# A re-ordered beginning for a four-layer graph network kernel on one core

## Chip, cores and metric

The kernel runs on one core of one Trainium2 chip. The metric is the device time of that core in microseconds (us), smaller is better. PE is TensorE (matmul), PEld its weight loads, DVE VectorE, ACT ScalarE, POOL GpSimd, SP SyncE; "SPq" and "ACTq" are the DMA queues that the sync engine and ScalarE issue to.

## The reference, cut to what matters

The input is 128 graphs of 128 nodes with 256 features. Four layers follow each other, each `x = layernorm(x + layer(x))`:

```python
x = _layernorm(x + L0(x, W_lin, W_val, a, W_out, adj, src, dst))   # attention over 512 edges
x = _layernorm(x + L1(x, adj, W1, W2, W3))                         # three mixes over adj * adj
x = _layernorm(x + L2(x, W, adj, bias))                            # diagonal, upper, lower part
x = _layernorm(x + L3(x, adj, ...))                                # batch norm over all graphs

# L0, for all graphs:
Xq = (H @ W_lin.T).reshape(bt, n, h, dh);  Xv = (H @ W_val.T).reshape(bt, n, h, dh)
e  = einsum('behd,hd->beh', leaky_relu(Xq[:, src] + Xq[:, dst]), a) + log(A0[src, dst] + EPS)
# softmax of e over the edges of equal src; then a sum over the edges of attn * Xv[:, dst], @ W_out.T
```

The edge list is the same for all graphs, so everything that depends on it alone is computed once: the **edge constants** (the order of the edges sorted by source, the gather indices, the log weight of each edge, the marks of repeated edges).

## The kernel before: the parts that matter

Graphs are processed in quads of four (32 quads). A quad's chain for layer 0 is: `values_in` (transposes), `values` (products with `wqv`, stored to DRAM as `qd`), `gather` (eight indirect DMAs on GpSimd, four plain ones by source, four that add by destination), `score` (VectorE), `softmax_parts` (four scans on VectorE), `attention`, `scatter` (four indirect DMAs, then a load of the whole attention matrix `ad`), `by_row` (copies on ScalarE) and `stage_a` (layer 0's matmuls and norm). A loop turn does stages of five different quads, in a fixed order of instructions per engine; ahead of the loop, the chains of quads 0 and 1 must have been run. In the code ahead of the loop the compiler's scheduler chooses the order; in the loop the written order is kept.

```python
a_sb = cload([P, N], "adj", adj)
xg0 = load_x(0, "xg", 1)
wqv = cload(...)
...
values_in(0, xg0)
for i in range(QB):
    values(0, i)
with tc.tile_pool(name="set", bufs=1) as sp:      # edge constants, in scratch memory of their own
    ...                                           # two 1 MB zero stores, ranks, permutation
    src_idx, dst_idx = ...                        # sorted gather indices
    ends_row = ...                                # the sorted ends, spread over all partitions
    for c in range(NE):                           # pairs of edges, on the sorted order
        nc.vector.tensor_scalar(same[:, c, :], pair_row, pair_col[:, c:c + 1], None, op0=ALU.is_equal)
        nc.vector.scalar_tensor_tensor(prior[:, c, :], ...)
        nc.vector.scalar_tensor_tensor(less[:, c, :], ...)
    nc.vector.reduce_sum(again, prior, axis=AX.X)
    ...                                           # log_row; adjacency: wt_t, split_t, diag_bc, ahat_t
cst2 = phase.enter_context(tc.tile_pool(name="cst2", bufs=1))
wo = cload(...); w1_sb = cload(...); w2_sb = cload(...); w3_sb = cload(...); l2w = cload(...) # 5.1 MB
...
gather(0)
edges(0)            # score and softmax of quad 0
whole(1)            # values_in and values of quad 1
attention(0)
scatter(0)
gather(1)
edges(1)
attention(1)
whole(2)
...
for j in range(QB):
    by_row(0, j)
scatter(1)
gather(2)
stage_a(0)          # layer 0 of quad 0
mix1(0, 0); mix1(0, 2); first(0, 0)
for i in range(QB): ... # first(0, i + 1), mix2(0, i)
with tc.manual_schedule(engines=None):
    for k in range(NQ + 1):
        iteration(k)
```

Of the kernel before, what the change touches and what calls it, by code (L numbers as in the profile page):

```python
# [19 lines left out]
BIG = 1e38  # L20
# [4 lines left out]
def gnn_stack(ctx: ExitStack, tc: tile.TileContext, x, adj, w_qv_t, a, w_out_t, src, dst,  # L25
# [80 lines left out]
    with ExitStack() as phase:  # L106
# [13 lines left out]

        a_sb = cload([P, N], "adj", adj)
        xg0 = load_x(0, "xg", 1)
        wqv = cload([P, DC, 2 * D], "wqv", w_qv_t.rearrange("(c p) f -> p c f", p=P))
        a_bc = cload([P, D], "a_bc", bass.AP(tensor=a.tensor, offset=a.offset, ap=[[0, P], [1, D]]), nc.scalar)

# [7 lines left out]
        log_row = ctile([R, E], "log_row", pool=cst)  # L133
# [11 lines left out]
        def values_in(k, xg=None):  # L145

            s = quads[k]
            s.xts = []
            xg = load_x(k, "xg", 1) if xg is None else xg
            for j in range(0, QB, 2):  # L150
                pt = ps("pt").rearrange("p (b c n) -> p b c n", b=2, c=DC)
                for t in range(2):
                    for c in range(DC):
                        nc.tensor.transpose(pt[:, t, c, :], xg[:, j + t, c * P:(c + 1) * P], ident)  # L154
                xt = ws.tile([P, 2, DC, P], F32, tag="xt", name="xt")
                nc.vector.tensor_copy(xt, pt)  # L156
                s.xts.append(xt)

        def values(k, i):

            s = quads[k]
# [7 lines left out]
            nc.vector.tensor_copy(s.xv[:, i, :], pq[:, D:])  # L169
            if i == QB - 1:  # L170
                s.qd = q_dram[k % 4]
                nc.sync.dma_start(s.qd, s.qt.rearrange("p b d -> p (b d)"))

        def gather(k):

            s = quads[k]
            s.z = [ws.tile([P, QB * D], F32, tag="zs", name=f"zs{k}_{c}", bufs=NE) for c in range(NE)]
            for idx, op in ((src_idx, ALU.bypass), (dst_idx, ALU.add)):
                for c in range(NE):
                    nc.gpsimd.indirect_dma_start(out=s.z[c], out_offset=None, in_=s.qd,  # L180
                                                 in_offset=bass.IndirectOffsetOnAxis(ap=idx[:, c:c + 1], axis=0),
                                                 compute_op=op)

        def score(k, c):
# [8 lines left out]
            nc.vector.reduce_sum(s.es[:, c, :], z.rearrange("p (r d) -> p r d", d=DH), axis=AX.X)  # L193

        def softmax_parts(k):
# [5 lines left out]
            e = wk.tile([R, E], F32, tag="e", name="e", bufs=1)  # L201
            nc.vector.tensor_add(e, log_row, pe[:R, :])
            yield
            f = wk.tile([R, E], F32, tag="f", name="f", bufs=1)
            nc.vector.tensor_tensor_scan(f, reset_f, e, initial=0.0, op0=ALU.add, op1=ALU.max)
# [5 lines left out]
            nc.vector.tensor_sub(e, e, m)  # L211
# [206 lines left out]


        values_in(0, xg0)  # L420
        for i in range(QB):
            values(0, i)
        with tc.tile_pool(name="set", bufs=1) as sp:
            src_col = cload([P, NE], "src_col", src.rearrange("(c p) -> p c", p=P), nc.scalar, I32, sp)
            dst_col = cload([P, NE], "dst_col", dst.rearrange("(c p) -> p c", p=P), nc.scalar, I32, sp)
            src_row = cload([P, E], "src_row", bass.AP(tensor=src.tensor, offset=src.offset, ap=[[0, P], [1, E]]),
                            nc.scalar, I32, sp)
            ones = ctile([P, P], "ones", pool=sp)
            nc.vector.memset(ones, 1.0)
            zero = ctile([P, N * R], "zero", pool=sp)  # L430
            nc.gpsimd.memset(zero, 0.0)
            for ad in att_dram:
                nc.scalar.dma_start(ad[:N * N, :].rearrange("(t s) r -> t (s r)", s=N), zero)


            pos = ctile([P, E], "pos", pool=sp)
            nc.gpsimd.iota(pos, pattern=[[1, E]], base=0, channel_multiplier=0,
                           allow_small_or_imprecise_dtypes=True)
            pos_col = ctile([P, NE], "pos_col", pool=sp)
            nc.gpsimd.iota(pos_col, pattern=[[P, NE]], base=0, channel_multiplier=1,  # L440
                           allow_small_or_imprecise_dtypes=True)
            ends = ctile([P, 2, NE], "ends", pool=sp)
            nc.vector.tensor_copy(ends[:, 0, :], src_col)
            nc.vector.tensor_copy(ends[:, 1, :], dst_col)
            key_row = ctile([P, E], "key_row", pool=sp)
            nc.vector.tensor_copy(key_row, src_row)
            nc.vector.scalar_tensor_tensor(key_row, key_row, float(E), pos, op0=ALU.mult, op1=ALU.add)
            key_col = ctile([P, NE], "key_col", pool=sp)
            nc.vector.scalar_tensor_tensor(key_col, ends[:, 0, :], float(E), pos_col, op0=ALU.mult, op1=ALU.add)

            less = ctile([P, NE, E], "less", pool=sp)
            rank = ctile([P, NE], "rank", pool=sp)
            perm = ctile([P, NE, E], "perm", pool=sp)
            bcast = ctile([P, 2, NE, P], "bcast", pool=sp)
            for c in range(NE):
                nc.vector.tensor_scalar(less[:, c, :], key_row, key_col[:, c:c + 1], None, op0=ALU.is_lt)
            nc.vector.reduce_sum(rank, less, axis=AX.X)
            for c in range(NE):
                nc.vector.tensor_scalar(perm[:, c, :], pos, rank[:, c:c + 1], None, op0=ALU.is_equal)
                for t in range(2):  # L460
                    nc.vector.tensor_copy(bcast[:, t, c, :], ends[:, t, c:c + 1].to_broadcast([P, P]))


            pc = ps("pcol")[:, :NE * 2].rearrange("p (c t) -> p c t", t=2)
            for c in range(NE):
                for i in range(NE):
                    nc.tensor.matmul(pc[:, c, :], perm[:, i, c * P:(c + 1) * P], ends[:, :, i],
                                     start=(i == 0), stop=(i == NE - 1))
            cols = ctile([P, NE, 2], "cols", pool=sp)
            nc.vector.tensor_copy(cols, pc)  # L470
            nc.vector.tensor_copy(src_idx, cols[:, :, 0])
            nc.vector.tensor_copy(dst_idx, cols[:, :, 1])

            ends_row = ctile([P, 2, E], "ends_row", pool=sp)
            for t in range(2):
                pr = ps("ends_ps")
                for c in range(NE):
                    nc.tensor.matmul(pr, bcast[:, t, c, :], perm[:, c, :], start=(c == 0), stop=(c == NE - 1))
                nc.vector.tensor_copy(ends_row[:, t, :], pr)


            pair_row = ctile([P, E], "pair_row", pool=sp)
            nc.vector.scalar_tensor_tensor(pair_row, ends_row[:, 1, :], float(N), ends_row[:, 0, :],
                                           op0=ALU.mult, op1=ALU.add)
            pair_col = ctile([P, NE], "pair_col", pool=sp)
            nc.vector.scalar_tensor_tensor(pair_col, cols[:, :, 1], float(N), cols[:, :, 0],
                                           op0=ALU.mult, op1=ALU.add)
            same = ctile([P, NE, E], "same", pool=sp)
            prior = ctile([P, NE, E], "prior", pool=sp)
            for c in range(NE):  # L490
                nc.vector.tensor_scalar(same[:, c, :], pair_row, pair_col[:, c:c + 1], None, op0=ALU.is_equal)
                nc.vector.scalar_tensor_tensor(prior[:, c, :], pos, pos_col[:, c:c + 1], same[:, c, :],
                                               op0=ALU.is_lt, op1=ALU.mult)
                nc.vector.scalar_tensor_tensor(less[:, c, :], pos, pos_col[:, c:c + 1], same[:, c, :],
                                               op0=ALU.is_gt, op1=ALU.mult)
            again = ctile([P, NE], "again", pool=sp)
            nc.vector.reduce_sum(again, prior, axis=AX.X)
            nc.vector.tensor_scalar(again, again, 0.5, None, op0=ALU.is_gt)
            spare = ctile([P, NE], "spare", pool=sp)
            nc.vector.scalar_tensor_tensor(spare, pos_col, float(N * N), pair_col, op0=ALU.add, op1=ALU.subtract)  # L500
            nc.vector.tensor_mul(spare, spare, again)
            nc.vector.tensor_add(spare, spare, pair_col)
            nc.vector.tensor_copy(att_idx, spare)
            count = ps("count")
# [289 lines left out]
```

## Time and profile before

| | before |
|---|---|
| median of 4 runs | 3486.15 us (3485.91 to 3490.95) |
| span of the profiled run, mean granted clock | 3483.9 us, 0.968 |
| busy: PE, DVE, ACT, POOL | 95%, 52%, 28%, 16% |
| first L314 matmul (loop proper starts) | 156.51 us |
| first split_t matmul of turn 1 (L359) | 230.42 us |

The prediction below shows and reads the table of stages, the matmul engine's waits and the queue lines. This is VectorE's timeline of the kernel before, with cuts. A row of a timeline is: start, length, engine, line, operation, tiles, shapes, count, and in brackets the idle time just before it with what ended it.

### The profile page before, as it was taken

The page shows a single profiled execution, that of the slowest core. Times are in us where ns is not written, and L with a number is a line of the kernel's source. Part 1 is how long each engine was busy: PE and PEld are TensorE (multiplying, and loading weights), DVE is VectorE, ACT ScalarE, POOL GpSimd, SP SyncE. Part 2 cuts the span into 40 slices and gives each one's busy share as a digit, 9 for nine tenths or more (in the row PEclk, how much of TensorE's full clock was granted, in tenths as well). Part 3 has the DMA queues.
Part 4 walks back from the last instruction along what each step waited for, and adds up shares of the span by engine and source line. Part 5 has one row for each costly group of instructions (what it writes and reads, how often), then busy time and mean ns, then how long its engine had stood idle before and what let it go on. Part 6 is the DMA issues. An engine that isn't in the chain of part 4 may idle for free.

```text
span 3483.9 us, 33805 instructions
## 1 busy us (share of the span) xinstructions
PE 3303.1 (95%) x13130; PEld 2105.6 (60%) x13130; DVE 1797.1 (52%) x3549; ACT 974.6 (28%) x1637; POOL 543.6 (16%) x460
## 2 busy tenths in 40 slices
PE   5599999999999999999999999999999999989963
PEld 2366666666666666666666666666666666654442
DVE  6544455555554555554445554555545553233379
ACT  1122222222222222222222222222222222234452
POOL 3211111111111111111111111111111110000000
PEclk8799999999999999999999999999999999999975
DMA  6433333323222233333333323322233331034446
GB/s 201 120 86 97 85 97 97 97 79 97 89 83 74 83 91 98 97 98 97 91 92 97 97 82 94 93 82 78 75 91 97 97 91 37 19 123 173 157 132 224
DMA packets 127743, 347.78 MB, mean 100 GB/s; under 512 B 14432, under 2 KB 68576, under 8 KB 115040
## 3 DMA queue, kind: packets, MB, share of 16 engines
q0 software_dynamic: 40960, 135.29, 16.1%
q1 hardware_dynamic: 65168, 190.53, 15.3%
q10 hardware_dynamic: 21456, 19.81, 1.7%
q8 instruction: 104, 1.70, 0.2%
q14 instruction: 55, 0.45, 0.0%
HBM read 258.55 MB, written 87.03 MB: 99 GB/s over the span
## 4 chain that ended last, share of the span: by engine, by line
PE 91%; DVE 4%; DMA 2%; issue 1%; ACT 0%; POOL 0%; DVEq 0%; POOLq 0%; ACTq 0%; SPq 0%
PE ph L314 25%; PE p L325 13%; PE po L373 10%; PE po L728 6%; PE ph L412 6%; PE ph L294 6%; PE pq L167 6%; PE pm L304 3%; PE po L269 3%; PE pm L359 3%; PE py L260 2%; PE pa L398 2%; PE pm L280 2%; PE po L336 2%; DVE x3l L98 1%
## 5 line engine op out<-in xcount | busy, mean ns | idle before, releaser
L314 PE MATMUL ph<-m,w 128*128 128x512 f32 x2048 | 887.2, 594 | 3.9 <-DVE m L305 3.9
L314 PEld LDWEIGHTS ph<-m,w 128*128 128x128 f32 x2048 | 390.5, 191 | 481.6 <-issue 476.0
L325 PE MATMUL p<-w,h 128*128 128x256 f32 x2048 | 450.4, 381 | 0.0
L325 PEld LDWEIGHTS p<-w,h 128*128 128x128 f32 x2048 | 387.1, 190 | 52.2 <-issue 0.5
L180 POOL DMA_INDIRECT zs<-qd,src_idx x128 | 126.5, 989 | 1797.6 <-DVE f L214 1571.8
L373 PE MATMUL po<-l2w,ms 128*128 128x256 f32 x1536 | 347.6, 379 | 1.2 <-DVE ms L365 1.2
L317 ACT ACTIVATE h<-ph 128x512 f32<-128x512 f32 x256 | 152.8, 597 | 598.6 <-PE ph L314 598.6
L373 PEld LDWEIGHTS po<-l2w,ms 128*128 128x128 f32 x1536 | 284.6, 190 | 35.9 <-DVE ms L365 1.4
L294 PE MATMUL ph<-w,mx 128*128 128x512 f32 x512 | 235.7, 593 | 0.0
L167 PE MATMUL pq<-wqv,xt 128*128 128x512 f32 x512 | 231.1, 605 | 2.9 <-DVE xt L156 2.9
L728 PE MATMUL po<-zl,l3w 128*128 128x512 f32 x512 | 221.9, 597 | 10.5 <-ACT zl L723 10.5
L412 PE MATMUL ph<-ag,l3w 128*128 128x512 f32 x512 | 225.5, 593 | 0.3 <-ACT ag L401 0.3
L180 POOL DMA_INDIRECT zs<-qd,dst_idx x128 | 202.8, 1584 | 121.5 <-DMA zs<-qd,src_idx 101.4
L338 DVE TENSOR_TENSOR xr<-xr,po 128x512 f32<-128x512 f32 x64 | 43.7, 683 | 336.5 <-PE po L336 336.5
L90 ACT ACTIVATE ln_sd<-ln_mv,eps 128x2 f32<-128x2 f32 x256 | 75.4, 294 | 456.5 <-DVE ln_mv L85 449.9
L156 DVE COPY xt<-pt 128x512 f32<-128x512 f32 x64 | 41.4, 685 | 310.1 <-PE pt L154 310.0
L236 POOL DMA_INDIRECT attd<-at,att_idx x128 | 127.5, 996 | 440.4 <-DMA attd<-at,att_idx 283.4
L98 DVE TENSOR_SCALAR xr<-xr,ln_mv,ln_rs 128x256 f32<-128x256 f32 x384 | 179.7, 510 | 6.9
L728 PEld LDWEIGHTS po<-zl,l3w 128*128 128x128 f32 x512 | 98.1, 192 | 134.3 <-issue 112.2
L190 DVE SCALAR_TENSOR_TENSOR zs<-zs 128x1024 f32<-128x1024 f32 x128 | 155.6, 1216 | 35.2 <-DMA zs<-qd,dst_idx 35.2
L412 PEld LDWEIGHTS ph<-ag,l3w 128*128 128x128 f32 x512 | 96.9, 190 | 121.6 <-issue 112.3
L167 PEld LDWEIGHTS pq<-wqv,xt 128*128 128x128 f32 x512 | 97.2, 195 | 115.1 <-issue 110.4
(173 smaller groups left out, 3965.4 us busy)
## 6 DMA issues: line engine op xcount, KB each, us to landing
ad<-attd SPq DMA_DIRECT2D x32, 1024.0 KB, 4.7
zd<-z SPq DMA_DIRECT2D x32, 1024.0 KB, 7.3
zl<-zd SPq DMA_DIRECT2D x32, 1024.0 KB, 4.8
xg<-in_x_dram SPq DMA_DIRECT2D x32, 512.0 KB, 4.2
qd<-qt SPq DMA_DIRECT2D x32, 512.0 KB, 2.6
xr<-in_x_dram SPq DMA_DIRECT2D x32, 512.0 KB, 5.8
x3d<-xr SPq DMA_DIRECT2D x32, 512.0 KB, 2.9
x3l<-x3d SPq DMA_DIRECT2D x32, 512.0 KB, 4.4
```

The costliest lines, as they stand in the source:

```text
L98: nc.vector.tensor_scalar(r[:, i, :], r[:, i, :], mv[:, i, 0:1], rs[:, i:i + 1], op0=ALU.subtract, op1=ALU.mult)
L167: nc.tensor.matmul(pq, s.xts[i // 2][:, i % 2, c, :], wqv[:, c, :], start=(c == 0), stop=(c == DC - 1))
L180: nc.gpsimd.indirect_dma_start(out=s.z[c], out_offset=None, in_=s.qd, in_offset=bass.IndirectOffsetOnAxis(ap=idx[:, c:c + 1], axis=0), com ...
L190: nc.vector.scalar_tensor_tensor(z, z, SLOPE, z, op0=ALU.mult, op1=ALU.max)
L236: nc.gpsimd.indirect_dma_start(out=ad, out_offset=bass.IndirectOffsetOnAxis(ap=att_idx[:, c:c + 1], axis=0), in_=s.at[:, c, :], in_offset= ...
L294: nc.tensor.matmul(ph, s.mx[i // 2 * 2][:, i % 2, dc, :], w1_sb[:, dc, :], start=(dc == 0), stop=(dc == DC - 1))
L314: nc.tensor.matmul(ph, w2_sb[:, c, f * P:(f + 1) * P], s.m2[:, c].rearrange("p b n -> p (b n)"), start=(c == 0), stop=(c == K1 - 1))
L317: nc.scalar.activation(h.rearrange("p b n -> p (b n)"), ph, AF.Relu)
L325: nc.tensor.matmul(p3[:, t * D:(t + 1) * D], s.h2[f][:, j + t, :], w3_sb[:, f, :], start=(f == 0), stop=(f == K2 - 1))
L373: nc.tensor.matmul(po[:, i % 2, :], mss[i][:, t, dc, :], l2w[:, t, dc, :], start=(n3 == 0), stop=(n3 == 3 * DC - 1))
L412: nc.tensor.matmul(ph, l3w1[:, dc, c * P:(c + 1) * P], s.ag[:, dc, :], start=(dc == 0), stop=(dc == DC - 1))
L728: nc.tensor.matmul(po, w2t[:, c, o * P:(o + 1) * P], z[:, c, :], start=(c == 0), stop=(c == K3 - 1))
```

## The change

The intent: run the start in an order written by hand (`start()` inside the manual schedule), with each load issued when it is needed. The edge constants are computed on the edges in their original order with accumulating compares, and only the needed results are sorted. Gather 0's eight pieces are interleaved, each add close behind its source piece, where the kernel before issues all four source pieces first. Quad 1's and quad 2's values run early, quad 3's leave turn 0, and layer 0 of quad 0 is placed ahead of the end of quad 1's chain. In the softmax an add of the log weights to the 16x512 scores becomes an add to the 128x64 ones, and in the loop the softmax steps stand at other places among the value products.

```diff
+        xg0 = load_x(0, "xg", 2)
+        wqv = cload(...)
         a_sb = cload([P, N], "adj", adj)
-        xg0 = load_x(0, "xg", 1)
-        wqv = cload(...)
... (gather)
+            if k == 0:
+                jobs = [(0, 0), (0, 1), (1, 0), (0, 2), (1, 1), (0, 3), (1, 2), (1, 3)]
... (score, softmax_parts)
+            if c == NE - 1:
+                nc.vector.tensor_add(s.es, s.es, log_col.unsqueeze(2).to_broadcast([P, NE, R]))
-            nc.vector.tensor_add(e, log_row, pe[:R, :])
... (iteration)
-            if has_g:
+            if has_g and not first_one:
                 values_in(g)
... (start; the "set" pool, its constants and the calls ahead of the loop are removed)
+            for c in range(NE):
+                nc.vector.tensor_scalar(less, key_row, key_col[:, c:c + 1], 0.0, op0=ALU.is_lt, op1=ALU.add,
+                                        accum_out=rank[:, c:c + 1])
+            ...                                   # perm; picked = adj[src, dst] by four small gathers
+            xg1 = load_x(1, "xg", 2)
+            nc.sync.dma_start(wo, ...); nc.sync.dma_start(w1_sb, ...)
+            nc.sync.dma_start(att_dram[0]..., zero)
+            nc.sync.dma_start(w2_sb, ...)
+            values_in(0, xg0, nc.scalar.copy)
+            for i in range(QB):
+                values(0, i, nc.scalar.copy, nc.scalar)
+            pc = sorted_columns(0)                # src_idx, dst_idx
+            gather(0)
+            ...                                   # pair constants on the original order
+            values_in(1, xg1, nc.scalar.copy)
+            for i in range(2):
+                values(1, i, nc.scalar.copy, nc.scalar)
+            pc = sorted_columns(2)                # att_idx, log_col
+            for i in range(2, QB):
+                values(1, i, nc.scalar.copy, nc.scalar)
+            ...                                   # keep and reset rows; second zero store; xg3
+            for c in range(NE):
+                score(0, c)
+            gather(1, ...)                        # into tiles that the loop needs later
+            ...                                   # softmax 0 with quad 2's values between its steps
+            attention(0)
+            scatter(0)
+            ...                                   # w3, l2w, bias, l3w1 loads; adjacency constants
+            gather(2)
+            for c in range(NE - 1):
+                score(1, c)
+            for j in range(QB):
+                by_row(0, j)
+            stage_a(0)
+            score(1, NE - 1)
+            values_in(3, xg3)
+            steps = softmax_parts(1)              # with values(3, i) between its steps
+            ...
+            attention(1)
+            scatter(1)
+            mix1(0, 0); mix1(0, 2); first(0, 0)   # then first and mix2 as before
```

## The prediction

> **What bounds the kernel now.** I read the page first: 3483.9 us of span with the matmul engine busy 95%, and slices that are full except at both ends. So I cut the beginning finely and gave each loop turn its own stretch. Columns: stretch, length, busy time of matmul, weight load, VectorE, ScalarE, GpSimd, granted clock, DMA share, GB/s.
> ```profile
> 0.00:156.50 156.50, 77.34 (x282) 43.88 (x282) 92.44 (x160) 21.66 (x34) 47.99 (x44) 0.76 0.62 179
> 156.50:187.00 30.50, 30.49 (x64) 13.29 (x65) 8.23 (x7) 7.03 (x10) 0.00 (x0) 0.90 0.00 1
> 187.00:202.40 15.40, 14.88 (x85) 9.24 (x83) 11.40 (x21) 7.00 (x11) 1.98 (x3) 1.00 0.14 50
> 202.40:230.40 28.00, 28.00 (x134) 21.51 (x134) 10.63 (x31) 5.50 (x11) 14.50 (x12) 1.00 0.66 155
> 230.40:323.80 93.40, 93.40 (x387) 60.88 (x386) 49.06 (x88) 25.44 (x43) 16.70 (x14) 1.00 0.35 104
> 323.80:417.00 93.20, 93.20 (x385) 60.68 (x385) 48.37 (x88) 25.54 (x43) 16.68 (x14) 1.00 0.32 91
> ```
> Two regimes. From 230.4 us a loop turn takes 93.2 to 93.4 us and the matmul engine has no gap: it is the bound. Before 156.5 us (the first L314 matmul, where the loop proper starts) it is busy 77 of 156 us; turn 0 runs from 156.5 to 230.4.
>
> Where do those 79 idle us go? The waits of the matmul engine from 0 to 160 us name it: (total, times, longest)
> ```profile
> PE pe L200 <- DVE es L193: 45.8, 6, 32.6
> PE half_ps L575 <- DVE half L573: 8.2, 1, 8.2
> PE pt L154 <- DMA xg<-in_x_dram: 7.3, 1, 7.3
> ```
> VectorE's scores in turn wait for gathers, so I read the timeline of GpSimd and of the sync queue.
> ```profile
> 25.26 1.11 POOL L180 DMA_INDIRECT zs<-qd,src_idx  x1 [21.48 <-DVE pair_col L486]
> 37.01 4.46 POOL L180 DMA_INDIRECT zs<-qd,dst_idx  x1 [0.30 <-issue]
> 73.84 1.03 POOL L236 DMA_INDIRECT attd<-at,att_idx  x1 [26.05 <-issue]
> 89.12 1.60 POOL L180 DMA_INDIRECT zs<-qd,dst_idx  x1 [0.30 <-issue]
> ```
> ```profile
> 54.19 0.37 SPq L111 DMA_DIRECT2D wo<-in_w_out_t_dram  x1
> 71.72 0.34 SPq L172 DMA_DIRECT2D qd<-qt  x1
> ```
> Quad 0's gather goes out at 25 to 41 us; quad 0's scatter and quad 1's gather only at 74 to 96, because the weights (5.1 MB, issued in a burst from 54 us when the set-up pool is released) stand ahead of quad 1's value store (71.7) in one queue. Then quad 1's whole chain runs, and quad 0's layer 0 (stage_a, first at 130.5) comes after it. From 73 to 104 us nothing computes.
>
> **What the Trainium skill says.** (1) "TensorE: Matmul & The Clock Gate", Part 1: the array falls to half clock after an idle window of about 3.4 us and needs about as much busy time to return. The trace agrees: granted clock 0.50 in 80:110, and after 3.85 us of idle the 64 matmuls of turn 0's L314 took 30.66 us, against 27.47 in turn 1. (2) "DMA: Bandwidth & Descriptors", "Issuing engines are not separate DMA queues": all share 16 engines, so a move to another queue brings order, not bandwidth. Here 60:70 us shows the engines full at 380 GB/s. (3) Same page, "Rules for kernel authors": an accumulating DMA must wait for the earlier one's semaphore. The trace shows 2.39 us of such a wait before one add-gather. (4) "ScalarE: Activation LUTs", "What ACT_TABLE_LOAD costs": 1283 ns; the trace has 1.28 us each.
>
> **The change, part by part.** The instruction order of both programs (built, not run) shows that the last 6925 of 7147 matmul instructions are the same, in the same order. So everything from turn 1 on should keep its 3253.5 us (3483.9 - 230.4), and the change is worth what it moves the start of turn 1. In the steady loop VectorE swaps a 16x512 add (0.68 us) for a 128x64 one (0.2 as the equally large L230): nothing, as it is busy 49 of 93 us. I walked the new in-order queues with durations of before (all new times are estimates):
>
> - Head. x comes first, without the 2 MB zero store beside it: transposes at 5.5 us (was 7.3). Transposes, copies on ScalarE and four value products (8.97 us for the products at 11.9 before): done at 16.5. The value store issues at 17; alone it lands in 2.6, beside 4.3 MB of loads in about 5: 22.
> - Indices. VectorE now needs key_row 0.69, four compares with accumulation (0.45 to 0.65 each), four perm (0.42), before 14 us. The 16 sorting matmuls follow the values: 3.63 us, so indices at 20.6. The edge constants no longer need the sorted rows; 8 wide products, bcast copies and two 2.3 us reductions vanish, but they were mostly beside other work. Gather 0 starts at 22 instead of 25.3.
> - Gather 0: eight transfers, issue 1.29 (source) or 1.85 (add) each = 12.6, about 2 of landing waits, last landing about 6: whole at 42 to 43. Interleaving lets scores start near 32, so only the last score (3 x 1.14 = 3.5) follows: 46.5. The constants (4 x (0.6+0.75), Ln with its table load) end near 28.5, before the scores; log_col adds 0.2.
> - Softmax of quad 0: transposes 0.6, four scans of 1.22, subtract 0.68, exp 0.64 and a table load of 1.28 in part, transposes 0.6, reciprocal and product 0.8 = 9.5: 56.
> - Quad 1's values wait behind the Ln on ScalarE (27.8), then run on a cold array with 3.6 of sorting amid them: stored at 42, landed 44.6. Gather 1 takes GpSimd to 58, ahead of scatter 0 in the same queue. **That is the new wait I expect**: scatter 0 starts at 58 instead of 73.8; its first piece queues behind the last gathers (to 64), three more at 2.5: 72. Load of the attention matrix, 5.5: 77.5.
> - Layer 0 of quad 0: by_row 4 x 0.99, last products, second half of L269, norm (add 0.69, stats 0.75, aggregate 0.3, root 0.3, apply 0.8): 88.5. I kept no gain for quad 0 being ready early: mix1(0) stands behind quad 1's softmax on the in-order matmul queue.
> - Quad 1's last score 3.5, two copies 1.3, softmax with quad 3's values between its steps 9 to 10: 103. Then mix1, first, mix2: before 138.44 to 156.51 = 18.1 with 3.85 waiting for VectorE; now free of it, 14.2. **Loop starts at 118** (was 156.5): 38.5 gained.
> - Turn 0. Quad 3's values leave it: 0.87 + 7.10 = 8.0 less. But they covered quad 2's softmax: stage_a's second copy stands behind the scans on VectorE, 7.3 + 0.7 us after L314, while the array has 4.6 of work: 3.5 exposed. From 15.4 the middle becomes about 10.6. L314 at full clock saves 3.2, a cold restart after the 3.5 of idle may cost 3: call it zero to 2. Turn 0: about 68 instead of 73.9.
>
> Turn 1 starts at 118 + 68 = 186 instead of 230.4. Sum: 186 + 3253.5 + 2.1 (timed over profiled span) = 3441.6. I add 2 us for waits that I did not see: **3444 us**, a gain of 42 or 1.2%.
>
> **The rivals.** (a) The freed loads collide elsewhere: w3, l2w and l3w1 (2.3 MB) are issued just behind the attention matrix and beside gather 2, and w2 beside gather 0. For it: ad<-attd took 8.9 us at 91.5 beside gathers, 4.7 in the median. Against it: what they feed starts over 60 us later, and ad is ahead in its queue. If each gather and the matrix lost 5: 3455 to 3462. (b) The serial chain through GpSimd (gather 1 ahead of scatter 0) and VectorE's late last score eat the reorder: if gather 1 waits longer for quad 1's store, every us goes to the end. 10 us more: 3454. (c) The chain is shorter: landings of 4 instead of 6 us (the fastest gather landed in 3.9), a warm array. Each of three gathers and five DMA steps gives 1 to 3: 3425 to 3432. (d) The matmul engine is the bound anyway and the start was hidden: against it stand 79 idle us before 156.5; excluded unless VectorE or ScalarE now stalls the loop, which equal streams and 49 of 93 busy us speak against.
>
> **Range and chances.** Errors of 5 us in each of three chain segments (gather 0 to scatter 0, scatter 0 to norm, softmax 1 to loop) add to about 9 us, and unseen order effects are more often losses: 3427 to 3461. Over 2% would need 3416.2, so the loop at about 92 us: less than the chain of about 22 + 20 + 13 + 16 + 5 + 11 + 14 + 14 us, three quarters of it transfers and VectorE. Chance 0.04. Slower by 2% needs a stall in every turn: 0.01.
>
> **What would show it right or wrong.** First gather near 22 us; scatter 0 near 58, right behind gather 1; first stage_a product near 79; first L318 (was L314) near 118; a gap of 3 to 4 us between turn 0's L318 and L329; first L363 near 186; turns of 93.2 to 93.4 from there. It is wrong if loop turns change length, if the first matrix load lands after 85, or if quad 1's softmax ends far from 103.

## More of the kernel before

```profile
39.98 2.28 DVE L497 TENSOR_REDUCE again<-prior 128x4 f32<-128x2048 f32 x1
...
46.42 1.20 DVE L190 SCALAR_TENSOR_TENSOR zs<-zs 128x1024 f32<-128x1024 f32 x1
...
95.03 1.23 DVE L190 SCALAR_TENSOR_TENSOR zs<-zs 128x1024 f32<-128x1024 f32 x1 [22.16 <-DMA zs<-qd,dst_idx]
```

The first score (L190 at 46.42) has no bracket: VectorE was at the edge constants until then and did not wait for gather 0, whose first finished piece had landed at 38.9 us. The first score of quad 1 (95.03) came after 22 us of idling for quad 1's gather.

## The result

| | before | after |
|---|---|---|
| median of 4 runs | 3486.15 us | 3449.39 us (3445.32 to 3453.88) |
| span of the profiled run, clock | 3483.9 us, 0.968 | 3446.5 us, 0.971 |
| first gather of quad 0 | 25.26 | 23.46 |
| scatter of quad 0 starts | 73.84 | 64.16 |
| first gather of quad 1 | 80.82 | 46.62 |
| first product of `stage_a` for quad 0 | 130.50 | 81.79 |
| loop proper starts (L314, now L318) | 156.51 | 126.42 |
| turn 1 starts (L359, now L363) | 230.42 | 192.88 |
| the rest of the span | 3253.5 | 3253.6 |

The ratio of after to before is 0.9892 with a 95% interval of 0.9874 to 0.9909: 1.1% faster, within 2%. Ratios in this text are the mean time of one kernel's fast runs over that of the other's of the same rounds, so not quite the ratio of the medians.

The gain of 37.5 us in the start of turn 1 came in three parts: 9.7 up to quad 0's scatter, 20.4 from there to the loop, 7.4 in turn 0.

The stages of the kernel after, with the columns of the prediction's first table:

```profile
0.00:126.40 126.40, 77.95 (x310) 46.39 (x310) 73.16 (x134) 29.67 (x57) 48.66 (x47) 0.80 0.75 223
126.40:154.15 27.75, 27.73 (x66) 12.31 (x67) 14.49 (x13) 7.04 (x10) 12.27 (x8) 1.00 0.63 157
154.15:165.10 10.95, 8.46 (x61) 6.81 (x60) 8.08 (x13) 4.22 (x6) 0.00 (x0) 0.84 0.19 36
...
192.88:286.10 93.22, 93.22 (x387) 60.63 (x386) 47.02 (x88) 25.46 (x43) 17.55 (x14) 1.00 0.32 89
```

The matmul engine does about the same work ahead of the loop (77.95 us for 77.34) in 30 us less; VectorE has 19 us less to do. Turn 0's long L318 group runs at full clock, and the middle of turn 0 is 4.5 us shorter. Turn 1 is what it was: 93.22 us without a gap.

The waits of the matmul engine in the first 130 us (total, times, longest):

```profile
PE pe L206 <- DVE es L199: 24.4, 2, 17.0
PE py L264 <- ACT adc L250: 10.8, 1, 10.8
PE pt L154 <- DMA xg<-in_x_dram: 5.5, 1, 5.5
```

The wait for the scores halved, from 45.8 to 24.4 us. In its place stands a new one: layer 0's first product waits 10.8 us for `adc`, which is the attention matrix on its way through DRAM.

Why the scores still wait is in VectorE's timeline of the kernel after, to be held against the one of before:

```profile
9.41 0.08 DVE L526 DVE_READ_ACCUMULATOR less<-key_row,small 128x1 f32 x1
...
37.05 1.22 DVE L194 SCALAR_TENSOR_TENSOR zs<-zs 128x1024 f32<-128x1024 f32 x1 [7.90 <-DMA zs<-qd,dst_idx]
...
94.41 1.22 DVE L194 SCALAR_TENSOR_TENSOR ag<-ag 128x1024 f32<-128x1024 f32 x1
```

The constants now end 7.9 us before gather 0 delivers. The bound of this stretch went from VectorE to the transfers. Two 10-us stretches of the same table show how busy the DMA engines were ahead of it:

```profile
10.00:20.00 10.00, 10.00 (x47) 6.01 (x47) 5.01 (x16) 2.59 (x8) 3.15 (x3) 0.95 1.00 379
20.00:30.00 10.00, 7.83 (x21) 2.85 (x20) 8.48 (x26) 3.67 (x7) 1.90 (x2) 0.88 1.03 390
```

The DMA engines are full (share 1.00 and 1.03) at 379 and 390 GB/s: `wo`, `w1`, two 1 MB zero stores, `w2` (2 MB) and x share them with quad 0's value store (7.1 us to land, where it took 2.6 before) and with gather 0. That accounts for the store, but not for the gather: from its first issue to its last landing gather 0 takes 27.2 us (23.46 to 50.62), in the kernel before 22.8 (25.26 to 48.04), and still 26.6 in the bandwidth experiment below, in which `w2` and a zero store are out of its way. What the traces show instead is GpSimd waiting for source pieces, each ahead of an add:

```profile
31.07 1.58 POOL L184 DMA_INDIRECT zs<-qd,dst_idx  x1 [5.40 <-DMA zs<-qd,src_idx]
...
40.18 1.54 POOL L184 DMA_INDIRECT zs<-qd,dst_idx  x1 [3.14 <-DMA zs<-qd,src_idx]
44.76 1.55 POOL L184 DMA_INDIRECT zs<-qd,dst_idx  x1 [3.04 <-DMA zs<-qd,src_idx]
```

These are 11.6 us in the interleaved order. In the kernel before no piece of gather 0 behind the first waited more than 0.30 us. No run takes the interleaving alone back, so its share of the 27.2 us is not shown.

The GpSimd timeline also shows quad 0's scatter, the step at which I expected a new wait:

```profile
46.62 0.97 POOL L184 DMA_INDIRECT z<-qd,src_idx  x1 [0.30 <-issue]
...
58.66 1.53 POOL L184 DMA_INDIRECT ag<-qd,dst_idx  x1 [0.30 <-issue]
64.16 1.02 POOL L240 DMA_INDIRECT attd<-at,att_idx  x1 [3.97 <-DVE at L234]
67.97 1.01 POOL L240 DMA_INDIRECT attd<-at,att_idx  x1 [2.80 <-DMA attd<-at,att_idx]
```

GpSimd had finished issuing gather 1 at 60.2 us and then waited 3.97 us for VectorE's `at`. The scatter starts when the softmax is done, not when the gather's issues are. But gather 1's last piece lands only at 67.5 us, just ahead of the scatter's second piece; the bandwidth experiment shows what that means.

### The profile page after: what moved, and what is told of

It reads as the page before. It is cut to its first block, busy times and chain, and to the rows that moved or that the text cites. A ratio compares the mean times of both kernels' runs of the same rounds, so it can differ in the third digit from the quotient of the medians.

```text
span 3446.5 us, 33811 instructions
## 1 busy us (share of the span) xinstructions
PE 3294.4 (96%) x13134; PEld 2102.9 (61%) x13134; DVE 1754.5 (51%) x3522; ACT 979.9 (28%) x1655; POOL 570.1 (17%) x463
## 4 chain that ended last, share of the span: by engine, by line
PE 93%; DVE 4%; DMA 2%; issue 0%; ACT 0%; POOL 0%; DVEq 0%; POOLq 0%; ACTq 0%; SPq 0%
PE ph L318 26%; PE p L329 13%; PE po L377 10%; PE po L736 6%; PE ph L416 6%; PE ph L298 6%; PE pq L168 6%; PE po L273 3%; PE pm L308 3%; PE pm L363 3%; PE py L264 2%; PE pm L284 2%; PE pa L402 2%; PE po L340 2%; DVE x3l L98 1%; DVE x3l L755 1%
## 5 line engine op out<-in xcount | busy, mean ns | idle before, releaser
L318 PE MATMUL ph<-m,w 128*128 128x512 f32 x2048 | 884.2, 592 | 0.8 <-DVE m L309 0.8
L318 PEld LDWEIGHTS ph<-m,w 128*128 128x128 f32 x2048 | 389.0, 190 | 477.1 <-issue 474.5
L184 POOL DMA_INDIRECT zs<-qd,src_idx x124 | 149.9, 1209 | 1729.6 <-DMA qd<-qt 1677.2
L184 POOL DMA_INDIRECT zs<-qd,dst_idx x124 | 192.5, 1553 | 143.8 <-DMA zs<-qd,src_idx 130.1
L98 DVE TENSOR_SCALAR xr<-xr,ln_mv,ln_rs 128x256 f32<-128x256 f32 x384 | 163.2, 467 | 6.9
L309 DVE COPY m<-pm 128x512 f32<-128x512 f32 x128 | 88.3, 690 | 147.2 <-PE pm L308 147.2
```

Source lines behind the costliest of these rows:

```text
L98: nc.vector.tensor_scalar(r[:, i, :], r[:, i, :], mv[:, i, 0:1], rs[:, i:i + 1], op0=ALU.subtract, op1=ALU.mult)
L184: nc.gpsimd.indirect_dma_start(out=s.z[c], out_offset=None, in_=s.qd, in_offset=bass.IndirectOffsetOnAxis(ap=idx[:, c:c + 1], axis=0), com ...
L318: nc.tensor.matmul(ph, w2_sb[:, c, f * P:(f + 1) * P], s.m2[:, c].rearrange("p b n -> p (b n)"), start=(c == 0), stop=(c == K1 - 1))
```

## The experiments

The questions were: which part of the change paid (the weights out of the way, quad 1's values early, shorter constants, quad 3's values moved), what the title's "layer 0 ahead of the second quad's chain" is worth, and what the start still loses. Twelve kernels ran, all with correct results. The first two calls ran on one chip (before took 3486.36 and 3487.38 us there); the third on another, on which before took 3535.61 us, also at the same granted clock. Times of the two chips are not compared, only ratios and, with care, landmarks of the start.

### The kernel after, again

No edit; it sets the spread. 

> The changed kernel once more, as the yardstick of this chip. First profile: turn 1 starts at 192.9 us, loop at 126.4; four times 3445 to 3454 us. Expected: 3449 us +- 3, the same landmarks within 3 us.

Measured: 3449.92 us, ratio 0.9888 (0.9873 to 0.9903). The loop starts at 128.48 us and turn 1 at 194.14, so landmarks of equal code differ by 1 to 2 us from run to run.

### Before, with the weights loaded early

```diff
 for i in range(QB):
     values(0, i)
+cst2 = ...            # the pool and the seven weight loads, unchanged
 with tc.tile_pool(name="set", bufs=1) as sp:
     ...
-cst2 = ...
```

My theory was that the burst of weights held up quad 1's store in the sync queue. The rival was that the order of the instructions held it up. 

> The kernel before with one thing changed: the weight tiles are allocated and loaded ahead of the set-up pool, so their 5.1 MB go out from about 6 us and not in a burst from 54 us. Theory A (my prediction's: the weights stood ahead of quad 1's store and held quad 0's scatter and quad 1's gather to 74-96 us): most of the gain comes with this alone, loop starts 25 to 30 us earlier (near 128), time near 3458 us. Rival B (the order of the quads' work is what cost: quad 1's values stood behind quad 0's score transposes on the in-order engines, its store was issued at 71.7 us the moment its data were ready, so the weights cost only the slower landings after it): loop starts 5 to 10 us earlier, near 148, time 3476 to 3481 us.

Measured: 3480.93 us, ratio 0.9981 (0.9968 to 0.9995). With the weights long loaded, quad 1's store in the sync queue goes out at the same time as in the kernel before (71.72):

```profile
71.52 0.34 SPq L172 DMA_DIRECT2D qd<-qt  x1
```

The theory was wrong: the queue was not what the store waited for. The loop starts at 149.11 us, 7.4 earlier, with the first gather of quad 1 at 74.97 instead of 80.82, which fits that gather and scatter no longer share the DMA engines with the weights; 5 us of that reach the end (the medians; 6.6 by the ratio, 2 to 11 by its interval). That is about a seventh of the gain.

### After, with quad 1's values put back

```diff
-values_in(1, xg1, nc.scalar.copy)
-for i in range(2): values(1, i, ...)
 pc = sorted_columns(2)
-for i in range(2, QB): values(1, i, ...)
 ...
-gather(1, ...)
 steps = softmax_parts(0)
-values_in(2, ...)      # quad 2's values were here
+values_in(1, ...)      # quad 1's values, as in the kernel before
 ...
 scatter(0)
+gather(1, ...)
+values_in(2, ...); values(2, i, ...)
```

> The changed kernel with one part undone: quad 1's value products, store and gather go back to where the kernel before has them, behind quad 0's score transposes and scatter 0 (quad 2's values after them); loads, edge constants and layer 0's place stay. Theory C (what the change gains is mainly that quad 1's store went out at 38 us and not at 72, so its gather and scores lie beside quad 0's): store near 67, gather 1 from 73 to 86, its scores end near 97 to 99, softmax 1 delayed: loop starts 8 to 15 us later than 126 to 128, time 3458 to 3464 us. Rival D (loads and edge constants carry the gain; quad 1's chain waits for layer 0 of quad 0 anyway): loop within 3 us, time 3450 +- 3.

Measured: 3460.69 us, ratio 0.9926 (0.9913 to 0.9938). Against 0.9888 for the unedited kernel, the difference of 0.0038 is 13 us (the medians differ by 11). The waits of the matmul engine in the first 140 us have a new second row, and the loop starts 8 to 10 us later:

```profile
PE pe L206 <- DVE es L199: 26.0, 2, 19.9
PE po L273 <- DVE yt L267: 12.7, 1, 12.7
```

Layer 0's second product waits 12.7 us for a copy on VectorE, which stands behind the late scores of quad 1. The edit also moves quad 2's values back, behind scatter 0. So the position of these values, and with it of gather 1 (73.45 here, 46.62 in the kernel after), is the largest part of the gain that a run here isolates.

### Constants: on the path before, off it after

Two kernels add about 4.6 us of reductions, without any use of their results, among VectorE's constants:

```diff
 # before
 nc.vector.reduce_sum(again, prior, axis=AX.X)
+nc.vector.reduce_sum(again, prior, axis=AX.X)
+nc.vector.reduce_sum(again, prior, axis=AX.X)
```
```diff
 # after
+for _ in range(2):
+    nc.vector.reduce_sum(src_wide[:, :, 0], perm, axis=AX.X)
 nc.vector.tensor_tensor(keep_f[:, 1:], src_row[:R, 1:], src_row[:R, :E - 1], op=ALU.is_equal)
```

> The kernel before with one reduction of its edge constants done three times (twice 2.28 us more on VectorE, same result): its first score starts at 46.4 us the moment VectorE is free, so if the edge constants were on the path there, the loop starts about 4.5 us later and the time is 3490 to 3491 us against 3486.5. If the later gather 1 hides it (its transfers, not the scores of quad 0, release the rest), under 1.5 us.

> The changed kernel with two reductions of the same size (2.28 us each, result unused) behind its edge constants, in VectorE's wait of 7.9 us for gather 0: if the change has taken the constants off the path, the loop starts when it did and the time is 3449.9 +- 2. If not, 4 to 5 us more, near 3454.

Measured, both on the second chip: before with more constants 3541.12 us, ratio 1.0016 (1.0003 to 1.003), 5.5 us over the median of before. After with more constants 3465.6 us, ratio 0.9802 (0.9789 to 0.9815). The unedited kernel after did not run on this chip, so the second is judged by its trace, VectorE's timeline:

```profile
27.05 4.60 DVE L594 TENSOR_REDUCE src_wide<-perm 128x4 f32<-128x2048 f32 x2
...
35.62 1.23 DVE L194 SCALAR_TENSOR_TENSOR zs<-zs 128x1024 f32<-128x1024 f32 x1 [1.95 <-DMA zs<-qd,dst_idx]
```

The 4.6 us go into the wait for gather 0 (7.90 us in the kernel after, 1.95 left here), and the softmax of quad 0 ends no later (`at` at 63.47, in the kernel after at 63.66); the loop starts at 126.29 us (126.42). In the kernel before, the same addition cost about its full length, within a wide interval (1 to 11 us), and the first score starts at 52.36 us where the unedited kernel, on the first chip, has 46.42. This fits constants that paid until VectorE met the gather, and no further; how much their shortening brought by itself no run shows.

### After, with quad 3's values back in turn 0

```diff
-first_one = k == 0
+first_one = False
 ...
-values_in(3, xg3)
 steps = softmax_parts(1)
-for i in range(QB):
-    next(steps)
-    values(3, i)
```

> The changed kernel with quad 3's value products put back into turn 0, where the kernel before has them. My prediction held that they cost about 4 us in the start and leave turn 0 by 8.0 less 3.5 to 4 of uncovered softmax, so that the move gains little: softmax 1 takes 8.5 us and not 12.9, loop starts near 123, turn 0 is 71 us and not 66.5; time 3449 +- 3. Rival (work moved into the idle start is free, all 8 us count): loop at 126 to 128 all the same, turn 0 at 74, time 3457.

Measured: 3453.71 us, ratio 0.9902 (0.9886 to 0.9917), 4 us over the unedited kernel. The loop starts at 124.35 us, 2 earlier than in the kernel after (4 earlier than in its repeat), and turn 0 takes 71.9 us instead of 66.5. Moving the values thus costs 2 to 4 us in the start and saves about 5 in turn 0. The time I expected (3449 +- 3) was missed by 2 us, and the intervals of the two ratios overlap.

### Layer 0 behind quad 1's chain, and the last score alone

The words of the change name layer 0 ahead of quad 1's chain. One kernel undoes just that:

```diff
-for c in range(NE - 1):
+for c in range(NE):
     score(1, c)
-for j in range(QB): by_row(0, j)
-stage_a(0)
-score(1, NE - 1)
 values_in(3, xg3)
 ...                   # softmax 1, values(3)
 attention(1)
+for j in range(QB): by_row(0, j)
 scatter(1)
+stage_a(0)
 mix1(0, 0)
```

(`xv` gets a fourth buffer, which this order needs, and two small tiles move into existing scratch memory to make room.) 

> The changed kernel with the order of its title undone: quad 1's last score, softmax (with quad 3's values between) and attention come first, then by_row and stage_a of quad 0 (one more buffer for xv, two scratch tiles shared to make room). Theory A (layer 0 of quad 0 ahead of quad 1's chain is a part of the gain): stage_a's 12.6 us (81.8 to 94.4) go to the end of the chain, loop starts about 10 later, near 136, time near 3459 us. Rival B (both pieces wait for each other in series on VectorE and TensorE either way, and VectorE idles before stage_a for the matrix load): the last score starts at 82.5 and not 94.4, the chain ends near 99, stage_a after it near 112, loop starts at 126 +- 2, time 3449 +- 3 us.

Measured: 3445.33 us, ratio 0.9879 (0.9864 to 0.9894): the median is 4.6 us *below* the kernel after, though the intervals overlap. The loop starts at 121.62 and turn 1 at 188.34, against 126.42 and 192.88 (128.48 and 194.14 in the repeat). A second kernel leaves layer 0 in front and moves only the last score of quad 1 ahead of it:

```diff
-for c in range(NE - 1):
+for c in range(NE):
     score(1, c)
 ...
-score(1, NE - 1)
```

> The changed kernel with one line moved: quad 1's last score ahead of stage_a of quad 0, in VectorE's wait of 3.4 us for the attention products (82.5 to 85.8), and not behind the norms (94.4 to 98.2). If, as predicted, that late score costs its full length: loop starts 3 to 3.7 us earlier, time near 3446 (3449.9 for the changed kernel, 3445.3 for e3, in which this move is contained). Rival (e3's gain comes from the warm attention products and the norm running beside mix1): within 1 us of the changed kernel.

Measured, on the second chip: 3461.84 us, ratio 0.9792 (0.9779 to 0.9805); turn 1 starts at 189.11 us, also 4 to 5 us earlier than in the kernel after. Both experiments fill the same hole. In the kernel after VectorE ends quad 1's third score at 82.5 us, idles 3.35 us for layer 0's first product and 2.00 us for the next, and turns to the last score only at 94.41, after layer 0's norm. Here is the start of the matmul groups concerned, first in the kernel after:

```profile
81.79 4.00 PE L264 MATMUL py<-adc,xv 128*64 128x128 f32 x32 [10.77 <-ACT adc L250]
...
99.27 9.58 PE L168 MATMUL pq<-wqv,xt 128*128 128x512 f32 x16
```

and then with layer 0 behind the chain, where quad 1's softmax runs while the attention matrix of quad 0 is on its way, and layer 0's first product waits for nothing:

```profile
86.06 9.34 PE L168 MATMUL pq<-wqv,xt 128*128 128x512 f32 x16
...
98.18 3.29 PE L264 MATMUL py<-adc,xv 128*64 128x128 f32 x32
```

On the second chip the nearest thing to the kernel after is after with more constants, whose loop starts where that of the kernel after does: it took 3464.24 to 3465.93 us and this kernel 3460.71 to 3462.78. So layer 0 ahead of the chain earned nothing that these runs show; as written, with a score behind it, it cost about 4 us.

### Bandwidth: w2 and the second zero store later

```diff
-nc.sync.dma_start(w2_sb, ...)                 # beside gather 0
-nc.sync.dma_start(att_dram[1]..., zero)
 ...
+nc.scalar.dma_start(att_dram[1]..., zero)     # behind quad 2's values
+nc.scalar.dma_start(w2_sb, ...)
 scatter(0)
```

> The changed kernel with two early transfers (w2, 2 MB, and the zeroes of the second attention matrix, 1 MB) issued from the ScalarE queue after quad 2's values, near 67 us, not at 8 to 20 us. Theory A (gather 0 ended 8 us later than predicted because the DMA engines are full from 10 to 35 us, 379 to 390 GB/s: the value store took 7.1 us for 2.6, source gathers 6.5 to 6.9): store 3 us, source gathers about 4, softmax 0 ends 7 to 9 us earlier (near 55), loop near 118, time near 3441 us. Rival B (gathers are slow of themselves, by what they move): landings change by under 1 us, loop near 126, time 3449 us; if w2 then comes too late, the loop waits for it and the time is longer.

Measured: 3450.29 us, ratio 0.9894, no difference. A part of the expected gain did come: quad 0's value store lands in 4.5 us instead of 7.1, gather 0 starts at 21.31 us instead of 23.46, and the softmax of quad 0 ends 2.6 us earlier (7 to 9 were expected). The gather itself hardly changed: 26.6 us from first issue to last landing, for 27.2. And the 2.6 us were given back at once. The GpSimd timeline of quad 0's scatter:

```profile
61.55 1.02 POOL L240 DMA_INDIRECT attd<-at,att_idx  x1 [1.67 <-DVE at L234]
67.97 1.01 POOL L240 DMA_INDIRECT attd<-at,att_idx  x1 [5.41 <-DMA attd<-at,att_idx]
74.62 1.03 POOL L240 DMA_INDIRECT attd<-at,att_idx  x1 [5.65 <-DMA attd<-at,att_idx]
```

The second piece starts at 67.97 us in both kernels, although the first went out 2.6 us earlier here; in both, gather 1's last piece had landed at 67.5. The third follows 6.65 us later (2.41 in the kernel after), with the zero store (landed at 70.98) and `w2` (76.41) now beside it, so the matrix load goes out at 79.19 us instead of 75.79. The loop starts at 126.64 us, as in the kernel after. Moving these two loads moved the collision.

### A better version

The experiments left two ideas: use VectorE's idle 7.9 us ahead of gather 0, and don't let layer 0 stand before scores. The first kernel takes the layer-0 order above and moves the adjacency constants (which stood between quad 0's `attention` and quad 1's scores) into the wait for gather 0, all but the last one, which goes behind quad 0's second score. The second also runs quad 3's values beside quad 1's scores, with copies on ScalarE, instead of between the softmax steps.

```diff
 # first: on top of "layer 0 behind quad 1's chain"
 for rs, kp in ((reset_f, keep_f), (reset_b, keep_b)): ...
+diag, an, own, sums, adj_t, diag_bc, wt_t, split_t, ahat_t = ...   # adjacency constants, here
 score(0, c) ...
-adj_t, wt_t, split_t, diag_bc, an, sums, ahat_t = ...              # not here, behind scatter(0)
```
```diff
 # second: on top of the first
-values_in(3, xg3)
-steps = softmax_parts(1)
+values_in(3, xg3, nc.scalar.copy)
 for i in range(QB):
-    next(steps)
-    values(3, i)
-for _ in steps:
+    values(3, i, nc.scalar.copy)
+for _ in softmax_parts(1):
     pass
```

> The version of e3 (quad 1's softmax ahead of layer 0 of quad 0, 3445.3 us) with the adjacency constants moved into VectorE's wait for gather 0 (29 to 37 us) from where they hold quad 1's first score until 71.3 us. If VectorE's queue is what sets the chain there, score 1 starts near 64 to 65 and everything after moves 5 to 7 us: loop near 116, time near 3439. If gather 1 is what sets it (its last piece lands near 67.6), the gain is 1 to 3 us: time 3442 to 3444.

> b1 with quad 3's value products put beside quad 1's scores and their PSUM copies given to ScalarE, so that softmax 1 has nothing between its steps: softmax 1 takes 8.5 us and not 13. If VectorE and TensorE queues set the chain: 3 to 4.5 us less than b1, time near 3435. If the load of quad 0's attention matrix (lands near 80) takes over: 0 to 2 us less.

Measured: 3437.95 us, ratio 0.9857 (0.9842 to 0.9872), and 3435.52 us, ratio 0.9851 (0.9836 to 0.9866). The second is the best of all on this chip, 51.9 us below before in its call. Its first score of quad 1 (VectorE's timeline) and its start of the loop:

```profile
63.33 1.22 DVE L194 SCALAR_TENSOR_TENSOR z<-z 128x1024 f32<-128x1024 f32 x1
```
```profile
112.52 27.73 PE L318 MATMUL ph<-m,w 128*128 128x512 f32 x64 [0.78 <-DVE m L309]
```

Quad 1's scores begin right after `at`, at 63.3 us instead of 71.3, and the loop starts at 112.5 instead of 126.4. The step from the first to the second, 2.4 us, lies within the intervals.

A third kernel spread the loads of the second still further (w2 behind the matrix load, the second zero store behind quad 1's values, the other weights behind scatter 1):

```diff
-nc.sync.dma_start(w2_sb, ...)                 # beside gather 0
 ...
+nc.scalar.dma_start(att_dram[1]..., zero)     # from ScalarE's queue, behind quad 1's values
 ...
 scatter(0)
-nc.sync.dma_start(w3_sb, ...); l2w, bias, l3w1
+nc.sync.dma_start(w2_sb, ...)
 ...
 scatter(1)
+nc.sync.dma_start(w3_sb, ...); l2w, bias, l3w1
```

> b2 (3435.5 us) with the late loads re-placed after what e4 showed: w2 goes out behind quad 0's attention matrix (near 77 us) and not at 8 us, the second zero store behind quad 1's value store (42 us), and the weights of the later layers only behind quad 1's matrix. If the early flood costs gather 0 about 3 us (e4: softmax 0 ended 2.6 us earlier) and nothing collides with scatter 0 this time (e4: two of its pieces took 6.4 and 6.7 us for 2.4): 2 to 4 us less than b2, near 3432.5. If w2 now delays gather 2, scatter 1 and its matrix past 119 us, turn 0 waits and it is slower than b2.

Measured, on the second chip: 3451.49 us, ratio 0.9763 (0.9749 to 0.9776). Its turn 1 starts at 179.26 us, the second's at 179.07, so the start shows no gain. Its lower ratio is not one either: it belongs to the chip, as the next part shows.

### What the second chip adds

On the first chip (and where the first comparison ran, with before at 3486 us as well) a turn takes 93.2 us in before, after and the best version alike. On the second, a turn of before with more constants takes 95.0 us, and one of the kernels with the new loop (last score alone, loads further spread) 93.8. These are the waits of the matmul engine from 1000 to 1475 us, five turns, of the first of them, and then of the kernel with the last score alone:

```profile
PE po L269 <- DVE yt L263: 5.4, 5, 1.1
PE po L269 <- ACT yt L263: 1.9, 5, 0.4
```
```profile
PE po L273 <- DVE yt L267: 1.8, 6, 0.3
```

On the first chip this view lists no wait at all for either kernel. Layer 0's output products wait for the copies of the mixed values, 1.5 us a turn in the old loop (of the 1.8 by which it is longer than on the first chip) and 0.4 of 0.6 in the new one. Vector and scalar operations last as long as on the first chip (the copy L263 692 ns on both), and a turn of the old loop has the same instructions in the same order as before's. From turn 1 to the end, before with more constants takes 3303.1 us there and after with more constants 3271.0, where before and after took 3253.5 and 3253.6 on the first chip. These 32 us are why kernels with the new loop show ratios near 0.98 there and near 0.989 here. Why the copies come later on that chip is open: no run isolates it, and the kernel after itself was not run there.

## Why the prediction was right, and where its steps were off

The predicted 3444 us was 5.4 below the measured 3449.39, inside the range of 3427 to 3461, and "within 2%" was right on the chip on which it was measured. The bound and the place of the gain were read rightly; that the sum came so close is in part luck, as errors of both signs met in it.

| step (us from the start) | predicted | measured |
|---|---|---|
| first transposes | 5.5 | 5.47 |
| gather 0 starts | 22 | 23.46 |
| gather 0 whole | 42 to 43 | 50.6 |
| scores of quad 0 done | 46.5 | 54.5 |
| softmax of quad 0 done | 56 | 63.9 |
| scatter 0 starts | 58 | 64.16 |
| attention matrix landed | 77.5 | 80.6 |
| norm of layer 0 done | 88.5 | 94.4 |
| softmax of quad 1 done | 103 | 112.5 |
| loop proper starts | 118 | 126.4 |
| turn 0 takes | 68 | 66.5 |
| the rest | 3253.5 | 3253.6 |

**Right.** The bound was read rightly: the loop could not change on that chip, and the whole change was the shift of turn 1's start, by 37.5 us where 44.4 were predicted. Turn 0 went as worked out: quad 3's products gone, L318 at full clock (27.73 us), and a gap in front of the products behind L264, though 2.49 us long and not 3.5. That layer 0's early place earns nothing, because `mix1` stands behind quad 1's softmax, fits the experiments, which even put it about 4 us worse, by the last score.

**The term that was mis-sized** is "Gather 0: … about 2 of landing waits, last landing about 6: whole at 42 to 43". GpSimd waited 11.6 us for landings and not 2; the three source pieces whose landing is in the trace took 6.5 to 8.4 us each, and each add must wait for its own. The last landing took 5.9 us, as predicted, and the scores were done 8 us later. About 1.5 of the 8 us came ahead of the gather: the value store was issued earlier than I had it (15.58 against 17) but landed in 7.1 us instead of 5. I had noted the rival (w2 and the zero store beside gather 0), but gave it no time in the sum; the bandwidth experiment shows that it is worth the 2.6 us of the store, and that the gather stays long without them (26.6 us). What is left by the traces is the interleaved order, which no run isolates. The trace of before could have warned me: there the same eight transfers took 22.8 us without such waits, and I allowed 20.6.

**A second, smaller term.** When the attention matrix landed, the delay was down to 3.1 us; from there to the loop it grew again to 8.4. Layer 0 of quad 0 took 13.8 us (80.6 to 94.4) and not 11, and the last score with softmax 1 took 18.1 us (94.4 to 112.5) and not 14.5. In both the array had idled before, which I counted for quad 1's values and for turn 0, but not here: the 32 value-mix products took 4.00 us after 10.8 us of idling, 1.97 in turn 0, and quad 3's value products 9.58 us after 7.4 of idling, 7.03 in a loop turn. The granted clock was 0.67 from 81.79 to 90.20 us and 0.73 from 99.27 to 108.80. The mixes after it (13.9 us, not 15), turn 0 and the margin of 2 us paid some of this back.

**The expected new wait did not come.** "That is the new wait I expect: scatter 0 starts at 58", right behind gather 1, fell: GpSimd waited 3.97 us for VectorE. As the softmax came 8 us late, GpSimd was free before it. The wait stood next in line, though: with the softmax 2.6 us earlier in the bandwidth experiment, the scatter's second piece did not move. Scatter and matrix load then took less than predicted, 16.4 us for 19.5, which gave 3 us back.

**The reading of before was wrong in one cause.** I wrote that scatter 0 and gather 1 were late "because the weights … stand ahead of quad 1's value store in one queue". With the weights out of the way the store still went out at 71.5 us. It was late because quad 1's values stood behind quad 0's scores in the order of instructions (their first copy on VectorE comes at 60.78 us, after the last score), and those behind VectorE's constants. The predicted time did not suffer, since I walked the new order step by step and took no gain from the weights. Smaller slips in the working: "nothing computes" from 73 to 104 us overlooks the score that VectorE does at 95.03; 103 and 14.2 make 117.2, written as 118; the chain's terms in the paragraph on the range add to 115; and 27.47 us for turn 1's L314 is from start to start, the row's own length is 27.63.

What is shown of the gain: 11 to 13 us by quad 1's values (with quad 2's moved along), 2 to 5 by quad 3's (not clear of the noise), constants that were on the path and are not, and 5 us for the weights in the kernel before. These are not independent, and they don't add to 37.5: about 10 us between scatter 0 and the loop are not assigned to a part by any run.

## What to carry to other kernels

When a start-up chain crosses engines and DMA, walk the new order event by event; but in a queue that works in order count every wait for the landing of an earlier piece (11.6 us here, for 2 predicted), and give a store that shares the DMA engines with loads its longer time (7.1 us here, for 2.6 alone). After each stretch in which the matmul engine idles, look at the clock it is granted before you price its next products. Before a queue is blamed for a late store, ask whether its data were there: the order of the instructions that make it may be the cause. And an operation that waits for a long transfer must not stand in front of work that is ready, not even on behalf of the item that is first in line.

## What the Trainium skill lacked or had wrong

- "DMA: Bandwidth & Descriptors" gives no cost of adding (accumulating) gathers or of what they share with loads. In the kernel after the DMA engines were 100% busy at 379 GB/s from 10 to 20 us, with stores and loads, and 81% busy at 181 GB/s from 30 to 40 us, 75 of the 81 with the gathers' queue: 379 against 223 GB/s for full engines (181 / 0.81). A 512 KB value store landed in 2.6 us alone and in 7.1 beside the loads; scatter pieces landed in 2.1 to 3.0 us, and one in 6.4 beside `w2`'s load and a zero store.
- "VectorE: DVE Perf Modes", "Two Vector instructions with no wait between them", says that an operation that writes its accumulator is two instructions. The trace agrees (a read of 0.08 us behind each), but the page doesn't say that the operation itself gets slower: a 128x512 compare took 0.75 us with accumulation, and 0.47 without (four in 1.86 us).
- No page that I read says that two chips can run the same loop at different lengths with full granted clock and equal operation times: 93.2 us a turn on one and 95.0 on the other for the old loop, 93.2 and 93.8 for the new one.
